# Two attention loops of a graph network: destinations' terms issued in the middle of a group, the rescaling factor issued behind the next sixteen slots' first scaling

## The chip, the cores and the metric

The kernel runs on one core of one Trainium2 chip. The metric is the device time of one execution in microseconds (us). Three runs of the kernel before took 5281.35, 5282.95 and 5290.66 us; their median is 5282.95. A profile of one further execution by the hardware profiler shows every instruction of the five engines: TensorE (PE, with its weight loads listed apart as PEld), VectorE (DVE), ScalarE (ACT), GpSimd (POOL) and SyncE (SP).

## The reference

The kernel computes four layers of a graph network over 3125 nodes with 256 features and 50,000 edges that are sorted by destination. Each layer normalises x, adds a graph part and a dense mixing part, and then a feed-forward part:

```python
edge_index = jnp.stack([src, dst])
xn = _layernorm(x, axis=-1)
x = x + _L0_gnn_ref(xn, edge_index, ...) + _L0_mix_ref(xn[None], ...)[0]
x = x + _L0_ffn_ref(_layernorm(x, axis=-1)[None], ...)[0]
...
```

The change touches the graph parts of layers 0 and 2 alone, which are graph attention: 4 heads of 64 features in layer 0, 8 heads of 32 in layer 2. Node features are multiplied by W, giving h. Each edge has, per head, a score: the source's term (h times att_src, summed over the head's features) plus the destination's term (h times att_dst), through a leaky ReLU of slope 0.2. A softmax over all edges that arrive at one node turns scores into weights, and the node's output is the weighted sum of the sources' h. A softmax needs each destination's maximum before the exponentials; that is what most of the loop below is about.

## The kernel before

**How the work is tiled.** The function `gat` holds the whole attention of one layer. The edges lie in 416 slots of 128 edges (one edge on each partition), each slot's edges having their destinations within one block of 128 nodes. Four slots make a group (`G` = 4, 104 groups), sixteen slots make a block of the loop (`J` = 16, 26 of them, four groups each; `b` is the block, `i` the group's place in it, 0 to 3). The sums for all nodes stay in SBUF in `agg`.

**What one group does.** `scale(g)` multiplies the group's gathered rows of h by the edges' weights (L836, DVE, one instruction of 128x1024; it reads the weights `weighed` from PSUM), copies the weights beside them (L837, ACT) and makes the one-hot matrices of the destinations (L556, DVE). `sums(g)` multiplies one-hot by rows, one matmul a slot (L845, PE), into a ring of PSUM tiles `g`, of which layer 0 has four and layer 2 three. `fetch(g + ring)` issues four gathers (L549, POOL, one indirect DMA a slot) of a later group. `add(g - 1)` adds the PSUM tiles of the group before to `agg` (L574, DVE).

**What one block of sixteen slots needs ahead of its first scaling.** Three pieces are prepared one and two blocks ahead:
- `terms(k)` gives the destinations' terms of half a block (eight slots): a DMA loads the destination rows into `dr` (L726, queued on SP; one buffer), DVE compares them into a transposed one-hot `ohT` (L729; one buffer), ACT copies eight pieces of the terms into `stage` (L732) and PE multiplies eight times (L735) into the PSUM tile `pd`. In layer 0 the two halves of `pd` and both blocks' `weighed` share one PSUM bank; in layer 2, with twice the heads, each half has a bank of its own (`per` is 2 and 1). `terms` for block b + 2 is issued in groups 0 and 1 of block b.
- `ready(b)` adds the three pieces that each term is split into (L743, DVE; L745, ACT) and loads the block's marks. It is issued in group 2, for block b + 2.
- `chain_of(b)` finds the running maximum over the sorted edges and ends in the weights. It is a generator with four stops: first the gathered sources' terms are copied together (L763, ACT, which needs the block's gathers landed), turned, scanned and turned back (L765 to L773); then the scan of the borders (L778 to L790); then the maxima (L794 to L800); then the exponential (L814, ACT), its copy into the PSUM tile `weighed` (L815, ACT) and the marks of the last edges (L816, DVE). Behind the last stop comes one instruction, L820 on DVE: the factor `goes`, by which the partial sum of a destination that continues from one block into the next must be rescaled, because the maximum may have grown. It reads the exponential.

`goes` is used in the first group of the next block: `sums` multiplies it with a one-hot matrix (L850, PE), and `add` applies the product to `agg` (L858 and L860, DVE) ahead of that block's first additions.

**What sets the order.** A scheduler gives each engine its list of instructions by the order of issue in the program text, and adds the semaphore waits. Each engine then runs its own list in that order: an instruction that waits holds everything behind it on its engine. So the places of the calls in the main loop of `gat` are the order written out by hand. After each group that is not the twelfth, `next(steps)` issues one step of the layer's dense mixing part (lines around L471, L473, L1049 to L1073 in layer 0, L1252 to L1267 in layer 2) into the same lists, to fill the holes.

In the kernel before, one turn of the main loop issues: `scale(g)`; in groups 2 and 3 one piece of the next block's chain; `sums(g)`, `fetch`, `add(g - 1)`; in group 1 the chain is started; in groups 1, 2 and 3 another piece of the chain, in group 3 the one that holds L820 alone; then in groups 0 and 1 `terms`, in group 2 `ready`; then a step of the mixing part.

Of the kernel before, what the change touches and what calls it, by code (L numbers as in the profile page):

```python
# [53 lines left out]
def bc(ap, shape):  # L54

    idx, full = [], []
    own = list(ap.shape)
    for n in shape:
        if n is None:
            idx.append(slice(None))  # L60
            full.append(own.pop(0))
        else:
            idx.append(None)
            full.append(n)
    assert not own
    return ap[tuple(idx)].to_broadcast(full)


class Net:
# [592 lines left out]
    def gat(self, pool, pre, H, tiny, side, ring, deg=None, after=None, head=None):  # L662
# [28 lines left out]
        nb, gb, ng = NS // J, J // G, NS // G  # L691
        state = {}
        heads = agg[:, :, :D].rearrange("p t (h c) -> p t h c", h=H)
        with ExitStack() as own:
# [15 lines left out]
            shares = [rp.tile([P, J + 1, 2 * H + 1], F32, name=f"alpha{i}") for i in range(2)]  # L710
# [10 lines left out]
            def terms(k):  # L721

                t0 = k * n
                dr = pool.tile([P, n, P], BF16, name="dr", bufs=1)
                rows = self.dl_rows[t0:t0 + n]
                nc.sync.dma_start(dr, bass.AP(tensor=rows.tensor, offset=rows.offset,  # L726
                                                           ap=[[0, P], [P, n], [1, P]]))
                ohT = pool.tile([P, n, P], BF16, name="ohT", bufs=1)
                nc.vector.tensor_scalar(ohT, dr, self.row, None, op0=ALU.is_equal)  # L729
                rows = pool.tile([P, n, 6 * H], BF16, name="stage")  # L730
                for j, r in enumerate(self.blocks_of(t0, n, ET.Activation)):
                    nc.scalar.copy(rows[:, j, :], dmf[:, bass.ds(r * (6 * H), 6 * H)])  # L732
                pd = pdt[k % 2 // per][:, k % per]
                for j in range(n):
                    nc.tensor.matmul(pd[:, j].rearrange("p s h k -> p (s h k)"), ohT[:, j, :], rows[:, j, :],  # L735
                                     start=True, stop=True)

            def ready(b):

                pds = pool.tile([P, J + 1, 2, H], F32, name="pds")  # L740
                for i, t in enumerate(pdt):
                    m = per * n
                    nc.vector.tensor_reduce(pds[:, i * m:(i + 1) * m], t.rearrange("p a j s h k -> p (a j) s h k"),  # L743
                                            axis=AX.X, op=ALU.add)
                nc.scalar.copy(pds[:, J], pds[:, 0])  # L745
                marks = rp.tile([M, 5 * P], F32, name="marks", bufs=2)
                rows = self.marks[b * J:(b + 1) * J]
                nc.sync.dma_start(marks, bass.AP(tensor=rows.tensor, offset=rows.offset,
                                                 ap=[[5 * P, J], [0, H], [1, 5 * P]]))
                state["in", b] = pds, marks  # L750
# [72 lines left out]
            def fetch(g):  # L823
                if g >= ng:
                    return
                msg = msgs.tile([P, G, W], F32, name="msg")
                for j in range(G):
                    self.gather(msg[:, j, :D + H], htab, g * G + j)
                state["msg", g] = msg

            def scale(g):
                msg = state["msg", g]
                b, s = g // gb, g % gb * G
                al_ = state["w", b][0]
                mh = msg[:, :, :D].rearrange("p j (h c) -> p j h c", h=H)
                nc.vector.tensor_tensor(mh, mh, bc(weighed[b % 2][:, s:s + G], [None, None, None, C]), ALU.mult)  # L836
                nc.scalar.copy(msg[:, :, D:], al_[:, s:s + G])  # L837
                state["oh", g] = self.one_hot(pool, g)

            def sums(g):  # L840
                oh, msg = state.pop(("oh", g)), state.pop(("msg", g))
                out = []
                for j in range(G):
                    q = ps.tile([P, 512], F32, name="g", bufs=room)[:, :W]
                    nc.tensor.matmul(q, oh[:, j, :], msg[:, j, :], start=True, stop=True)  # L845
                    out.append(q)
                state["q", g] = out
                if g and g % gb == 0:
                    q = mm()
                    nc.tensor.matmul(q[:, :H], oh[:, 0, :], state["w", g // gb][1], start=True, stop=True)  # L850
                    state["less"] = q[:, :H]

            def add(g):
                if g and g % gb == 0:
                    less = state.pop("less")
                    at = agg.rearrange("p t w -> p (t w)")[:, bass.ds(self.block_of(g * G, ET.DVE) * W, D + H)]
                    ah = at[:, :D].rearrange("p (h c) -> p h c", h=H)
                    nc.vector.scalar_tensor_tensor(ah, bc(less, [None, None, C]), 1.0, ah, op0=ALU.add, op1=ALU.mult)  # L858
                    ad = at[:, D:]
                    nc.vector.scalar_tensor_tensor(ad, less, 1.0, ad, op0=ALU.add, op1=ALU.mult)  # L860
                self.add_group(agg, g, state.pop(("q", g)))
# [10 lines left out]
            for g in range(ng):  # L872
                b, i = divmod(g, gb)
                scale(g)
                if i > 1 and b + 1 < nb:
                    next(links)
                sums(g)
                fetch(g + ring)
                if g:
                    add(g - 1)  # L880
                if i == 1 and b + 1 < nb:
                    links = chain_of(b + 1)
                if i and b + 1 < nb:
                    next(links, None)
                if b + 2 < nb:
                    if i < 2:
                        terms(2 * (b + 2) + i)
                    elif i == 2:
                        ready(b + 2)
                if g % 12:  # L890
                    next(steps, None)
            add(ng - 1)
# [1709 lines left out]
```

## Time and profile before

| | us |
|---|---|
| median of three runs | 5282.95 |
| the profiled execution's own time | 5287.8 |
| its span, first to last instruction | 5286.0 |
| busy in the span: PE, DVE | 4213.0, 3243.5 |
| busy in the span: POOL, ACT | 2038.9, 1470.6 |
| loop of layer 0, about 155 to 757 of the span | 602 |
| loop of layer 2, about 2930 to 3563 of the span | 633 |
| L836 in both loops, 208 instructions of 1.211 each | 252.0 |
| L845 in both loops, 1664 matmuls of 0.453 each | 576.9 |
| L549 in both loops, 832 gathers of 0.997 each | 829.4 |

The TensorE clock that the throttle granted was 0.883 of full speed on average over the span, 0.89 in layer 0's loop and 0.93 in layer 2's. "Idle before" or "waits" means time in which an engine had nothing running, put down to whatever released the next instruction: `DVE msg L836 <- PE pd L735` is DVE standing still ahead of line 836, which makes `msg`, until line 735 on PE, which writes `pd`, was done. In the timeline each line has the start in the span, the duration, engine, line, operation and tiles, and in square brackets the engine's idle time ahead of it. The two loops do not overlap each other or the rest of the program by more than their edges.

### The profile page before, as it was taken

Reading aid. Unit: us, or ns where it says so; the run is one execution under the profiler, and the core shown is the slowest. Engines: PE = TensorE matmul, PEld = TensorE weight load, DVE = VectorE, ACT = ScalarE, POOL = GpSimd, SP = SyncE. Lnnn points to the kernel's source line nnn. Section 1 sums busy time; section 2 is a strip of 40 time slices with the busy share of each in tenths; the row PEclk is TensorE's granted clock in tenths of the full one; section 3 lists DMA queues with packets and bytes.
Section 4 is the critical chain, followed back from the end, with each engine's and each line's share of the span. In section 5 each row is a group of like instructions: output and inputs, shape, how many; then the busy total and the mean of one; then the engine's idle time right before and its main releaser. Section 6 shows DMA issues by size and latency. Waiting matters only on the chain. (4 is left out here: it accounts for less than half of the span.)

```text
span 5286.0 us, 70446 instructions
## 1 busy us (share of the span) xinstructions
PE 4213.0 (80%) x20470; PEld 3023.8 (57%) x20470; DVE 3243.5 (61%) x7881; ACT 1470.6 (28%) x4893; POOL 2038.9 (39%) x2048
## 2 busy tenths in 40 slices
PE   4788864977777766776795688886999999995996
PEld 2444534864654344554683444555756777775996
DVE  6888787137898467997415787887565443473112
ACT  2323334232100322334222333325342111112232
POOL 1766631426777266771241666641020000001221
PEclk8888885987897788887797799998999999997998
DMA  4544433664454256773464444431023542345554
GB/s 118 137 116 111 113 85 105 190 164 129 144 154 144 74 176 191 226 228 110 128 192 131 126 122 120 118 107 47 6 86 91 184 115 72 87 121 180 175 171 156
DMA packets 395084, 693.86 MB, mean 131 GB/s; under 512 B 88252, under 2 KB 230342, under 8 KB 394689
## 3 DMA queue, kind: packets, MB, share of 16 engines
q1 hardware_dynamic: 288594, 414.48, 25.3%
q0 software_dynamic: 95744, 264.11, 18.0%
q10 hardware_dynamic: 10351, 10.60, 0.6%
q8 instruction: 176, 2.88, 0.2%
q14 instruction: 219, 1.79, 0.1%
HBM read 572.82 MB, written 116.15 MB: 130 GB/s over the span
## 5 line engine op out<-in xcount | busy, mean ns | idle before, releaser
L549 POOL DMA_INDIRECT msg<-L_gnn_htab,src x832 | 829.4, 997 | 566.4 <-issue 332.5
L549 POOL DMA_INDIRECT msg<-L_gnn_c_tab,src x832 | 823.8, 990 | 451.0 <-issue 321.1
L617 PE MATMUL g<-msg,oh 128*128 128x256 f32 x1664 | 554.3, 468 | 267.2 <-DVE agg L574 162.0
L574 DVE TENSOR_TENSOR agg<-agg,g 128x256 f32 (+2 forms) x1664 | 697.5, 419 | 110.3 <-PE g L617 55.6
L845 PE MATMUL g<-msg,oh 128*128 128x265 f32 (+1 forms) x1664 | 576.9, 453 | 131.9 <-DVE agg L574 102.1
L617 PEld LDWEIGHTS g<-msg,oh 128*128 128x128 f32 x1664 | 341.4, 227 | 415.4 <-DVE agg L574 229.7
L1605 DVE COPY y<-y 128x256 f32<-128x256 f32 x162 | 68.8, 425 | 714.9 <-PE y L1602 714.9
L845 PEld LDWEIGHTS g<-msg,oh 128*128 128x128 f32 x1664 | 302.0, 207 | 325.4 <-DVE agg L574 221.9
L1561 POOL DMA_INDIRECT xr<-L_ffn_rows,takes x162 | 155.8, 962 | 791.5 <-PE tx L1570 401.9
L1589 PE MATMUL h<-xe,w 128*128 128x128 f32 x3456 | 418.7, 278 | 2.7 <-DMA w<-in_L_ffn_W 2.7
L1593 ACT ACTIVATE hT<-h,br 128x128 f32<-128x128 f32 x864 | 247.1, 368 | 618.2 <-issue 548.0
L1602 PE MATMUL y<-w,hT 128*128 x1728 | 416.2, 389 | 0.0
L1589 PEld LDWEIGHTS h<-xe,w 128*128 128x128 f32 x3456 | 405.4, 194 | 3.4 <-issue 3.2
L2286 DVE CAST ar<-a 128x640 fp32r<-128x640 bf16 x500 | 254.0, 509 | 223.2 <-PE dn L2288 219.1
L2288 PE MATMUL dn<-ha,ar 128*128 128x512 f32 x1500 | 383.7, 407 | 5.1 <-DVE ha L2253 3.4
L1602 PEld LDWEIGHTS y<-w,hT 128*128 128x128 f32 x1728 | 314.9, 190 | 55.4
L2288 PEld LDWEIGHTS dn<-ha,ar 128*128 128x128 f32 x1500 | 279.0, 189 | 82.5 <-issue 8.9
L836 DVE TENSOR_TENSOR msg<-msg,pd 128x1024 f32<-128x1024 f32 x208 | 252.0, 1211 | 36.9 <-PE pd L735 27.1
L2288 PE MATMUL dn<-hb,ar 128*128 128x512 f32 x1000 | 258.9, 413 | 13.4 <-DVE ar L2286 13.4
L2219 ACT ACTIVATE T<-mm 128x512 bf16<-128x512 f32 (+1 forms) x280 | 151.1, 550 | 361.1 <-PE mm L2217 360.9
L1407 POOL IOTA slot<- 128x56 f32 x3 | 0.9, 294 | 637.9 <-ACT ha L2382 561.7
L1606 POOL DMA_INDIRECT back<-y,puts x162 | 160.6, 991 | 179.6 <-DVE y L1605 138.5
(734 smaller groups left out, 7213.4 us busy)
## 6 DMA issues: line engine op xcount, KB each, us to landing
a<-counted SPq DMA_DIRECT2D x500, 160.0 KB
w<-in_L_ffn_W SPq DMA_DIRECT2D x124, 512.0 KB
w<-in_L_ffn_W SPq DMA_DIRECT2D x62, 1024.0 KB
counted<-T SPq DMA_DIRECT2D x40, 800.0 KB
dr<-dl_rows SPq DMA_DIRECT2D x104, 256.0 KB
heavy_oh<-oh SPq DMA_DIRECT2D x104, 256.0 KB
oh<-heavy_oh SPq DMA_DIRECT2D x104, 256.0 KB
msg<-L_gnn_htab,src POOLq DMA_INDIRECT x832
```

Source lines behind the costliest of these rows:

```text
L549: self.nc.gpsimd.indirect_dma_start(out=out, out_offset=None, in_=table, in_offset=bass.IndirectOffsetOnAxis(ap=self.src[:, t:t + 1], axis=0))
L574: self.nc.vector.tensor_tensor(at, at, q[j], ALU.add)
L617: self.summed = self.nc.tensor.matmul(r, oh[:, j, :], msg[j], start=True, stop=True)
L836: nc.vector.tensor_tensor(mh, mh, bc(weighed[b % 2][:, s:s + G], [None, None, None, C]), ALU.mult)
L845: nc.tensor.matmul(q, oh[:, j, :], msg[:, j, :], start=True, stop=True)
L1561: nc.gpsimd.indirect_dma_start(out=xr, out_offset=None, in_=tab, in_offset=bass.IndirectOffsetOnAxis(ap=takes[:, t:t + 1], axis=0))
L1589: nc.tensor.matmul(q[:, i, :], d["w1"][:, k, c * P:(c + 1) * P], d["xe"][:, k, :], start=(k == 0), stop=(k == 1))
L1593: nc.scalar.activation(hT[:, c, :], q[:, i, :], act, bias=d["br"][:, c:c + 1])
L1602: nc.tensor.matmul(q, d["hT"][:, c, :], w2f[:, bass.ds(e * (nh * D) + c * D, D)], start=False, stop=(c == nh - 1))
L1606: s = nc.gpsimd.indirect_dma_start(out=self.back, out_offset=bass.IndirectOffsetOnAxis(ap=puts[:, t:t + 1], axis=0), in_=y, in_offset=None)
L2286: nc.vector.tensor_copy(r, a)
L2288: nc.tensor.matmul(q.rearrange("p i f -> p (i f)"), r[:, k, :], of(h, k0 + k).rearrange("p i f -> p (i f)"), start=(k0 + k == 0), stop=(k0 ...
```

## The change

Three things change in `gat`. `scale` takes the block's weights from the list `shares` by the block's number, where it took them from the record that the last piece of the chain leaves; it is the same tile. The last piece of the chain, the factor `goes` (L820), is issued in group 0 of the next block, behind that group's `scale`, where it was issued at the end of group 3 ahead of it. And `terms` is issued between `scale` and `sums` of groups 0 and 1, where it was issued at their end, behind `sums`, `fetch` and `add`. The pieces of the chain in groups 1, 2 and 3 and `ready` in group 2 stay where they were.

```diff
@@ scale(g)
                 msg = state["msg", g]
                 b, s = g // gb, g % gb * G
-                al_ = state["w", b][0]
+                al_ = shares[b % 2]
@@ the main loop
                 scale(g)
                 if i > 1 and b + 1 < nb:
                     next(links)
+                elif b and i == 0:
+                    next(links, None)
+                if i < 2 and b + 2 < nb:
+                    terms(2 * (b + 2) + i)
                 sums(g)
                 fetch(g + ring)
                 if g:
                     add(g - 1)
                 if i == 1 and b + 1 < nb:
                     links = chain_of(b + 1)
-                if i and b + 1 < nb:
-                    next(links, None)
-                if b + 2 < nb:
-                    if i < 2:
-                        terms(2 * (b + 2) + i)
-                    elif i == 2:
-                        ready(b + 2)
+                if i in (1, 2) and b + 1 < nb:
+                    next(links)
+                if i == 2 and b + 2 < nb:
+                    ready(b + 2)
                 if g % 12:
                     next(steps, None)
```

## The prediction

> **What bounds the kernel now.** First the page's busy shares and its chain of what ended last, to see whether the two attention loops matter; then busy time in the stretch of each loop; then what DVE, PE, ACT and POOL wait for in those stretches; last the timeline of one block's turn in each. The page and the two stretches:
>
> ```profile
> span 5286.0 us, 70446 instructions
> PE 4213.0 (80%) x20470; PEld 3023.8 (57%) x20470; DVE 3243.5 (61%) x7881; ACT 1470.6 (28%) x4893; POOL 2038.9 (39%) x2048
> ...
> 155.00:757.00 602.00, 499.39 (x2078) 276.66 (x2078) 493.85 (x1199) 186.87 (x844) 374.97 (x383) 0.89 0.42 114
> 2930.00:3563.00 633.00, 522.60 (x2240) 320.11 (x2238) 519.84 (x1289) 203.07 (x979) 382.68 (x384) 0.93 0.44 119
> ```
>
> In the two lower lines the columns are length, then busy time of PE, weight loads, DVE, ACT and POOL, clock, DMA share, GB/s. Layer 0's loop takes 602 us and layer 2's 633, together 1235 of 5286; only they change. In both PE and DVE are each busy 82 to 83%: neither bounds alone. They hand work to each other, and a wait of one tells only if the other has nothing queued. The waits of DVE (total, times, longest), layer 0 above, layer 2 below:
>
> ```profile
> DVE msg L836 <- PE pd L735: 26.2, 22, 3.4
> DVE goes L820 <- ACT alpha L814: 9.2, 7, 3.1
> ...
> DVE goes L820 <- ACT alpha L814: 47.8, 22, 3.9
> DVE ohT L729 <- DMA dr<-dl_rows: 1.2, 3, 0.5
> DVE msg L836 <- PE pd L735: 0.8, 2, 0.6
> ```
>
> The two waits that the change is next to: the scaling L836 held by the terms' matmuls L735 (layer 0 alone, where both halves of the terms and the factors `weighed` are in one PSUM bank; layer 2 has two banks and 0.8 us), and the rescaling factor L820 held by the exponential L814 (layer 2 above all). One turn of a block in layer 2:
>
> ```profile
> 3227.09 0.22 ACT L763 COPY mine<-msg 128x32 f32<-128x32 f32 x1 [3.18 <-DMA msg<-L_gnn_htab,src]
> ...
> 3228.11 0.31 ACT L814 ACTIVATE alpha<-z 128x136 f32<-128x136 f32 x1
> 3228.45 0.17 DVE L820 SCALAR_TENSOR_TENSOR goes<-alpha,goes 128x8 f32<-128x8 f32 x1 [1.58 <-ACT alpha L814]
> 3228.68 0.26 ACT L815 COPY pd<-alpha 128x128 f32<-128x128 f32 x1
> 3229.22 1.21 DVE L836 TENSOR_TENSOR msg<-msg,pd 128x1024 f32<-128x1024 f32 x1
> 3231.45 0.33 PEld L850 LDWEIGHTS mm<-goes,oh 128*128 128x128 f32 x1
> ```
>
> L836 needs L815, which ends at 3228.94, 0.52 us after L814. So the exponential that L820 waits for is also on the way to L836. And ACT itself is late because the gather's landing is (3.18 us). That is a cycle: L836 opens the old block's last sums, these free the buffers of POOL's next gathers, they land, and the next exponential follows. A block takes 24.9 us here, 24.0 in layer 0, with 25 turns each.
>
> **The change part by part.** Instruction for instruction the five engines run what they ran before (104 calls of `terms`, 52 factors); only the order moves. The scaling's other name for the factor tile costs nothing, it is the same tile.
>
> *The terms, moved ahead of the sums, layer 0.* A call of `terms` issues one 256 KB DMA on SP's queue, one DVE compare L729 (0.48 us), eight ACT copies L732 (0.21 us each) and eight matmuls L735. They used to stand at the end of groups 0 and 1, so the next group's scaling came soon behind them and had to wait out the same bank: DVE stood 26.2 us, 22 times. In the new order, on PE the first half's L735 run right after the old block's last four sums matmuls, before the group's own sums; the second half's after the sums of the block's first group. On DVE the work between the second half's compare and the following scaling rises from 1.3 us to about 3.5; between the first half's and its scaling it is 0.7 to 1.6, as now. So the second half's wait goes and the first half's is shortened only by what PE no longer has ahead of it. From the present stalls, block by block, I estimate 0.2 to 0.45 us a block left over; 25 x 0.44 = 11. Term: 11 - 26.2 = -15 (bounds -26.2, all gone, and 0, where sums that are late take its place on PE).
>
> Ahead of this stands PE: its sums wait for the adds (50.4 us, 75 times), so L735 in that place uses PE time that was often idle; eight take 0.35 us in one row of the timeline, with 0.47 of weight loads beside them. If PE had no hole there, it would be 50 x 0.5 = 25 us the other way, and I keep that for the range.
>
> *The terms' DMA.* The destination rows have one buffer, so the next load is issued when the compare L729 has read it. Measured from issue to landing in the trace it takes 3.05 to 4.07 us, mostly about 3.5. Now 4.1 to 8.6 us of DVE work stand between the two compares, and the wait is 1.2 us in layer 2 and absent in layer 0. In the new order I count only 3.1 us of it in 9 blocks of layer 0 and 3.1 to 3.8 in 6 of layer 2. Each then waits 0.3 to 0.5 us: 9 x 0.45 = +4 and 6 x 0.35 = +2 (bounds 0, and 15 x 1.0, the slowest landing less the shortest work: +15). The page "DMA: Bandwidth & Descriptors" of the Trainium skill, section "Anatomy of one DMA", would fit 2.0 us plus bytes over 436 GB/s, an estimate of 2.6 us for 256 KB, on the gpsimd path; by it nothing would wait, this term would be 0 and the forecast 5266. Its rule "issue the DMA early, wait late" (section "Rules for kernel authors") speaks against the change, which pulls the two compares together. The trace's 3.5 us decides.
>
> *The factor L820, behind the first scaling.* DVE no longer stands at L820; it stands at L836 instead, until L815 is done 0.26 to 0.5 us after L814, and what stood between the two (side work, an add) is run during the wait. Going through the blocks with the trace's own end times, the stall sum is 11.8 -> 10.9 us in layer 0 and 52.1 -> 49.5 in layer 2 (both include short stalls that the list puts elsewhere). Terms -0.9 and -2.6, instead of the -57.0 that the list of waits would promise.
>
> Queued behind the moved L820 is PE's L850, which multiplies the factor, and behind it the group's side matmuls. The factor is now done 1.21 + 0.17 = 1.38 us or more after the scaling starts. L850 needs the one-hot L556 too, which comes after the scaling both before and after (it is what PE waits for: 5.1 us in layer 2), so mostly L850 was not ready earlier. It bounds at 0 and 25 x 1.38 = +34.5; I take 0, nearest to the row above, where L850 runs 2.2 us after L836's start, and later than the factor would be.
>
> *The terms in layer 2.* No bank is shared, so nothing is gained at L836 (0.8 us at most). What counts is whether L735 delays the old block's last sums, which release POOL. By the order on PE, the eight stand ahead of the last of them in some of the block patterns: +0.5 us in two, +0.8 in three, -1 in two where a side matmul moves behind, the rest unchanged. Over the loop that is -3 to +5: +1.
>
> Sum: layer 0, -15 + 4 - 0.9 = -11.9; layer 2, -2.6 + 2 + 1 = +0.4; together -11.5. The profiled execution took 5287.8 us (span 5286.0 and 1.8 around it), so 5276.3 for it; the median of the three runs is 4.85 lower, so **5271.5, say 5272 us**. About 0.2%, 10.6 us, is what a measurement of this kernel can tell from no change: the forecast is at that edge.
>
> **The rivals.**
> *The waits only change hands: 5283.* For it: L820's wait does so by the working above, and PE and DVE being busy 83 and 82% means that a stall taken from DVE can come back as a stall of PE on the adds (50.4 us now). Against it: 26.2 us of one wait at one bank are not work. It gives -11.5 + 11.5, no change.
>
> *All of it is gained: 5249.* The wait of 26.2 goes entirely, layer 0's 0.9 too, and in layer 2 the scaling starts as L815 ends, 0.28 us earlier a block as in the timeline, and the whole cycle with it: 25 x 0.28 = 7. 34 off: 5253.8 - 4.85. Against it: the first half has no more cover on DVE than now.
>
> *Slower: 5306.* The place is layer 2's turn of a block. PE is in order; L850 waits for the factor 1.38 us after the scaling's start, and terms and sums behind it wait too, so that the gathers' release is late by as much in each of 25 blocks: +34.5 - 11.9 = +22.6. For it: POOL sat idle in 5 us pieces there and ACT waits 63.5 us on landings, so the cycle has no slack. Against it: the one-hot, which L850 needs as well. It cancels layer 0's gain from 0.48 us a block on, and is slower past the bound from 0.9.
>
> **How the numbers follow.** Likeliest case, partial gain (5260 to 5283): 0.38, of which 0.23 below 5272.4, 0.12 within the bound and 0.03 past it, where the transfer's bound of +15 comes in. All gained: 0.18. Hands changed: 0.14. Slower by the cycle or by PE's missing hole: 0.30. Hence faster 0.41, within 0.26, slower 0.33. The range reaches into the full gain and the slower case, 5246 to 5306; the likeliest one's own is 5260 to 5283.
>
> **What the profile after would show.** In layer 0 the wait of L836 on L735 falls from 26.2 to about 11; near 26 says that the move does not get the matmuls out of the way, near 0 the full gain. The wait of L820 on L814 vanishes in both loops and a wait of L836 on L815 of about 45 to 50 us stands in layer 2; if it is far under 40, the cycle has become shorter than I think. L729 waits on its DMA for 4 to 8 us where it was 1.2. Layer 2's length tells the slower rival: 633 -> 650 or more, with POOL's idle time grown and PE waiting at L850 on L820. The prediction is wrong if the stall taken from DVE in layer 0 appears on PE, L845 on L574, above 60.

## The result and the profile after

The changed kernel took 5298.51 us (median of 8 runs, 5285.72 to 5311.52), the kernel before 5283.25 us in the 8 runs beside it (5267.59 to 5298.72). The ratio is 1.0028 with a 95% interval of 1.0015 to 1.0042: some 15 us slower, where 11 us faster was forecast. The profiled execution of after took 5311.5 us, the longest of its eight; the first of the two lines below is the page's, the others are busy time in the two loops, each from its first scaling L836 to its last (length, then PE, weight loads, DVE, ACT, POOL, granted clock, DMA share, GB/s).

```profile
span 5309.7 us, 70468 instructions
...
157.80:766.60 608.80, 509.57 (x2079) 279.86 (x2080) 496.20 (x1202) 187.28 (x848) 380.02 (x383) 0.87 0.42 113
2949.90:3589.20 639.30, 525.41 (x2237) 329.21 (x2235) 517.56 (x1288) 202.06 (x978) 380.38 (x384) 0.91 0.43 118
```

Between the same instructions, layer 0's loop took 603.5 us before and 608.8 after, layer 2's 631.7 and 639.3: +5.3 and +7.6. Of the profiles' difference of 23.7 us another 11.0 lie between the loops (2172.3 and 2183.3 us), where the change moves nothing; so one execution differs from the next by that much. The loops' 12.9 are near the 15 of the medians, but each is one execution. DVE does the same work as before (496 and 518 us). PE is busy 10 us longer in layer 0, with the same matmuls, at a granted clock of 0.87 where it was 0.89.

The waits of DVE, then of PE, in layer 0's loop after; then of DVE and of PE in layer 2's (total, times, longest). The windows are those of the two lines above:

```profile
DVE msg L836 <- PE pd L735: 17.1, 16, 4.0
DVE msg L836 <- ACT pd L815: 13.0, 11, 3.1
...
DVE ohT L729 <- DMA dr<-dl_rows: 2.0, 5, 0.5
...
PE g L845 <- DVE agg L574: 62.0, 83, 4.0
...
DVE msg L836 <- ACT pd L815: 22.6, 9, 4.4
DVE goes L820 <- ACT alpha L814: 19.8, 7, 4.7
...
DVE ohT L729 <- DMA dr<-dl_rows: 4.0, 7, 1.1
...
PE pd L735 <- DVE ohT L729: 14.1, 7, 3.4
...
PE mm L850 <- DVE goes L820: 6.0, 6, 2.0
```

Before, PE's rows for the same two waits were, in layer 0's loop and in layer 2's:

```profile
PE g L845 <- DVE agg L574: 50.4, 75, 2.2
...
PE pd L735 <- DVE ohT L729: 2.0, 2, 1.1
```

In layer 0 the scaling's wait for the terms fell from 26.2 to 17.1 us, and PE's wait for the adds rose from 50.4 to 62.0. In layer 2 the wait for the exponential is split between L820 and L836, 42.4 us together, where it was 48.1 before (47.8 at L820, 0.3 at L836). New is PE standing at L735: 14.1 us on L729, where before it stood 2.0. These matmuls now have sums behind them.

The lists that the engines run do not follow the order of issue alone, as I had it ahead of the change: the scheduler places instructions earlier or later than the program text does. So the edit moves less than it says. In layer 2 the factor L820 still runs ahead of the scaling in 7 of 25 turns (in layer 0 in 3), and these 7 are the whole 19.8 us. Of the 48 calls of `terms` in a loop, the first L735 runs 2 to 8 of the sums' matmuls earlier than before in 45 calls of layer 0, but only in 27 of layer 2, there by 2 to 6.

Where the longest blocks come from is seen in one place of the timeline. After, the turn into block 11 of layer 2 (POOL's idle time at the end counts from its last gather):

```profile
3227.22 0.22 ACT L763 COPY mine<-msg 128x32 f32<-128x32 f32 x1 [4.89 <-DMA msg<-L_gnn_htab,src]
3227.35 0.38 ACT L1253 ACTIVATE qk<-mm 128x256 f32<-128x256 f32 x1
...
3228.21 0.17 DVE L1254 TENSOR_SCALAR s<-s 128x2 f32<-128x2 f32 x1 [4.63 <-ACT qk L1253]
3228.36 0.44 DVE L574 TENSOR_TENSOR agg<-agg,g 128x273 f32 x1
...
3228.86 1.28 PE L845 MATMUL g<-msg,oh 128*128 128x273 f32 x2 [3.83 <-DVE agg L574]
...
3234.32 2.08 PE L473 MATMUL mm<-L_mix_W_qkv,xT 128*128 128x512 f32 x2
...
3238.05 0.94 POOL L549 DMA_INDIRECT msg<-L_gnn_htab,src  x1 [8.48 <-issue]
```

ACT stands 4.89 us at a copy L763, which waits for a gather to land. Behind it in ACT's list is a square of the mixing part, behind that in DVE's list an add, and behind that PE's sums: all four stop. PE then runs at half clock (two of the matmuls L473 take 2.08 us; four of them took 1.98 at 3220.86, at full clock). The stretch in the middle has the clock in the last column but two:

```profile
3220.00:3228.00 8.00, 4.88 (x17) 2.56 (x17) 3.49 (x12) 1.30 (x8) 5.99 (x7) 1.00 0.62 176
...
3232.00:3238.00 6.00, 6.00 (x13) 3.34 (x12) 1.91 (x4) 0.00 (x0) 0.00 (x0) 0.50 0.00 0
```

PE is busy all of these 6 us and POOL has nothing, since the old block's sums, which free its buffers, come through at half speed. Its next gather starts 9.26 us after the scaling (6.90 in the same block before), so it lands late, and the next L763 waits for such gathers. Blocks 5 and 11 take 29.6 and 29.8 us, before 26.5 and 26.8.

### The profile page after: what moved, and what is told of

Its sections match the earlier page's. It is cut to its first block, busy times and chain, and to the rows that moved or that the text cites. A ratio compares the mean times of both kernels' runs of the same rounds, so it can differ in the third digit from the quotient of the medians.

```text
span 5309.7 us, 70468 instructions
## 1 busy us (share of the span) xinstructions
PE 4234.7 (80%) x20470; PEld 3041.7 (57%) x20470; DVE 3242.7 (61%) x7881; ACT 1469.1 (28%) x4893; POOL 2041.0 (38%) x2048
## 3 DMA queue, kind: packets, MB, share of 16 engines
q1 hardware_dynamic: 288594, 414.48, 25.3%
## 5 line engine op out<-in xcount | busy, mean ns | idle before, releaser
L836 DVE TENSOR_TENSOR msg<-msg,pd 128x1024 f32<-128x1024 f32 x208 | 252.1, 1212 | 55.5 <-ACT pd L815 35.6
L2289 PEld LDWEIGHTS dn<-hb,ar 128*128 128x128 f32 x1000 | 192.8, 197 | 65.9 <-DVE ar L2287 21.9
```

What stands on the lines that cost most here:

```text
L2289: nc.tensor.matmul(q.rearrange("p i f -> p (i f)"), r[:, k, :], of(h, k0 + k).rearrange("p i f -> p (i f)"), start=(k0 + k == 0), stop=(k0 ...
```

## The experiments

Ratios are to the kernel before on the same chip, with 95% intervals. Loops are from the first to the last scaling, of one profiled execution each; executions of one loop that nothing was changed in differ by up to 9 us (layer 2 unchanged: 631.7 and 623.0), so a smaller difference of single loops says little. "Half clock" is the time in layer 2's loop at a granted clock of 0.5.

| kernel | ratio | layer 0 | layer 2 | half clock |
|---|---|---|---|---|
| before | 1 | 603.5 | 631.7 | 82 |
| after | 1.0028 [1.0015, 1.0042] | 608.8 | 639.3 | 110 |
| e1 terms alone | 1.0020 [1.0007, 1.0033] | 596.3 | 638.6 | 99 |
| e2 factor alone | 0.9978 [0.9967, 0.9990] | 605.6 | 608.9 | 59 |
| e3 both, layer 0 alone | 1.0000 [0.9986, 1.0014] | 595.0 | 623.0 | 80 |
| e4 both, layer 2 alone | 1.0034 [1.0015, 1.0053] | 607.3 | 651.8 | 136 |
| e5 after, L735 behind the sums | 1.0002 [0.9992, 1.0012] | 586.9 | 631.5 | 89 |
| e6 factor, terms in layer 0 | 0.9961 [0.9948, 0.9975] | 596.4 | 606.8 | 54 |
| e7 after, L763 behind L814 | 0.9878 [0.9863, 0.9894] | 590.4 | 590.5 | 61 |
| e8 factor, L763 behind L814 | 0.9860 [0.9845, 0.9875] | 591.9 | 583.7 | 51 |
| e13 after, step shifted | 1.0050 [1.0032, 1.0068] | 599.5 | 641.5 | 109 |
| e14 factor, step shifted | 1.0034 [1.0021, 1.0048] | 600.7 | 644.0 | 132 |
| e15 before, L763 behind L814 | 0.9874 [0.9854, 0.9894] | 591.3 | 588.1 | 59 |
| e16 e6, L763 behind L814 | 0.9871 [0.9851, 0.9891] | 593.8 | 586.6 | 54 |

**Which part.** e1 moves the terms alone, e2 the factor alone; e3 and e4 do both in one loop.

```diff
 e1, on before
                     next(links)
+                if i < 2 and b + 2 < nb:
+                    terms(2 * (b + 2) + i)
                 sums(g)
...
-                if b + 2 < nb:
-                    if i < 2:
-                        terms(2 * (b + 2) + i)
-                    elif i == 2:
-                        ready(b + 2)
+                if i == 2 and b + 2 < nb:
+                    ready(b + 2)
 e2, on after: the same lines the other way
 e3 and e4, on after: the two moves only where moved is true
+            moved = H == 4        # e4: H == 8
```

> Only the terms are moved between the scaling and the sums; the factor L820 stays at the end of the block's last group. Theory A (the terms' matmuls, now ahead of the sums on PE, make the sums wait for the compare L729 and the copies L732): this alone gives nearly the whole loss, +10 to +16 us on before, and PE's waits of L735 on L729 and of L845 on L732 stand as in the changed kernel (14 us in layer 2, 5 us in layer 0). Theory B (the loss is the factor's new place): 0 to -10 us. Theory C (no single part: every reordering that lengthens PE's holes lowers the granted clock): the half-clock time grows with the loss.

> Only the factor L820 is moved behind the next block's first scaling; the terms stay at the end of groups 0 and 1. Theory A: -4 to +3 us on before. Theory B (L850 waits for the factor, and what stands behind it): +10 to +16 us, with PE's wait of L850 on L820 at 6 us or more.

> Both parts in layer 0's loop alone, where before the scaling waited 26 us on the terms' matmuls in the shared bank. My forecast of the place had -12 us here. From the profile of the changed kernel, whose loop is 5 us longer than before, +5 us; if the time of the loops' surroundings is noise, then layer 0 alone is +3 to +7 us.

> Both parts in layer 2's loop alone, where nothing waits on a shared bank. From the profile of the changed kernel, whose loop is 7.6 us longer, +6 to +10 us; with the run before it the sum of the two should be the loss of the changed kernel, +15 us.

The terms alone cost 11 us of 5286.3 (interval 4 to 17), the factor alone gains 12 (5 to 17). So theory B falls, and the loss is the terms'. By layer, e3 is no change (+3 to +7 was expected) and e4 is +18 us (8 to 28; 6 to 10 was expected): the loss is layer 2's. But theory A had 14 us of PE at L735 on L729 in layer 2 for e1 too, and there it is 6.4. The waits that carry this, of e2 in layer 2 (its L820 and L836 as in the changed kernel):

```profile
DVE msg L836 <- ACT pd L815: 17.9, 8, 3.3
DVE goes L820 <- ACT alpha L814: 17.8, 9, 3.4
...
PE pd L735 <- DVE ohT L729: 2.4, 2, 1.5
```

With the factor alone DVE stands 35.7 us for the exponential, where it stood 48.1 before (47.8 at L820, 0.3 at L836), and layer 2's loop is 23 us shorter. In e4 both parts in the same loop give 651.8. The two parts don't add: the factor gains where the terms stay, and loses its gain where they move. Theory C's sign is there in the first six rows: layer 2's half-clock time, 59 to 136 us, goes up and down with its loop. e1 speaks against a loss by the squares qk of the mixing part (the narrow form of theory D, below): there none of them stands behind L763, and layer 2's loop is as long as the changed kernel's (638.6 and 639.3).

**Is it L735 ahead of the sums?** e5 leaves the load, the compare and the copies of the terms in the new place and issues the eight matmuls behind the sums again. e6 moves the factor in both loops and the terms in layer 0 alone.

```diff
 e5, on after: terms becomes a generator
                 for j, r in enumerate(self.blocks_of(t0, n, ET.Activation)):
                     nc.scalar.copy(rows[:, j, :], dmf[:, bass.ds(r * (6 * H), 6 * H)])
+                yield
                 pd = pdt[k % 2 // per][:, k % per]
...
                 if i < 2 and b + 2 < nb:
-                    terms(2 * (b + 2) + i)
+                    rest = terms(2 * (b + 2) + i)
+                    next(rest)
                 sums(g)
...
                 if i in (1, 2) and b + 1 < nb:
                     next(links)
+                if i < 2 and b + 2 < nb:
+                    next(rest, None)
 e6, on after: early = H == 4; terms ahead of sums where early, else at the end
```

> The changed kernel with each terms call cut in two: its load, compare L729 and copies L732 stay between the scaling and the sums, its eight matmuls L735 go back behind the sums, the additions and the chain's piece. Theory A (the loss is L735 ahead of the sums on PE): the loss of +15 us goes, 0 to -10 us on before, and PE's wait of L735 on L729, 14 us in layer 2, falls under 4. Theory D (the loss is on ACT: in blocks 5 and 11 of layer 2 the side work's squares qk now stand behind the four copies L763, which wait for gathers that land late, and DVE, PE and POOL follow): ACT's list has the same place for them here, so +10 to +16 us stays.

> The factor behind the first scaling in both loops, the terms moved in layer 0 alone. The profiles of the runs so far have layer 0's loop at about 600 us with the terms moved and 605 without, and layer 2's at 609 with the factor alone: -12 to -18 us on before. If the terms' place is bad in either loop, it is no better than the factor alone: -11.

e5 is at 1.0002: the loss is gone, as theory A has it, and the gain of the factor has not come back. But it is a weak test of L735's place. In PE's list the matmuls run later than in the changed kernel in only 8 of 48 calls of layer 2 and in 10 of layer 0. PE's wait at them on L729 in layer 2 fell from 14.1 to 6.4 us, not under 4, and its wait at L850 on L820 rose from 6.0 to 12.1. Layer 2's loop, 631.5, is still 22.6 above e2's. And most of the shortening stands in layer 0's loop (608.8 to 586.9), where e3 shows no loss; no run explains that. So L735's place can be one part of the loss, and how large a part stays open. e6 is 0.9961, 21 us faster than before (13 to 28), the best ratio that the two moves give, though its interval overlaps e2's.

e6 and the changed kernel differ only in the terms of layer 2: 0.9961 against 1.0028, each to the kernel before on its own chip. So the terms' new place costs some 35 us there (25 to 45) once the factor is moved.

**Is it the queue behind L763?** In ACT's list the next block's four copies L763 stand ahead of the exponential L814 of the block at hand, though they are issued later in the program: in layer 2 in nearly every block, before and after, in layer 0 in a few early blocks and in all but the last from the eleventh on. The timeline shows ACT held there by landings. The row before, in layer 2's loop:

```profile
ACT mine L763 <- DMA msg<-L_gnn_htab,src: 63.5, 23, 4.1
```

In the changed kernel two of the four squares qk stand behind them in blocks 5 and 11 besides. e7 and e8 turn the order of L763 and L814 round, in after and in e2, and compute the same:

```diff
                 nc.vector.scalar_tensor_tensor(zs, zs, 0.2, zs, op0=ALU.mult, op1=ALU.max)
-                z = pool.tile([P, J + 1, H], F32, name="z", bufs=1)
+                z = mine[:, 0]
                 nc.vector.tensor_tensor(z, zs[:, 0], zs[:, 1], ALU.subtract)
```

L814 now reads `mine`, and L763, which writes it, can't go before.

> The changed kernel, but the exponential's input z is written into the tile mine where it had a tile of its own, so that the next block's four copies L763, which overwrite mine, must stand behind L814 on ACT, where now they stand ahead of it and hold it until late gathers have landed. The same work, nothing left out. Theory D: the waits of the factor and of the scaling on ACT (48 us in layer 2) go nearly all, layer 2's loop falls by 30 to 50 us, and the terms' place does no more harm: -30 to -50 us on before. Theory A: L735 ahead of the sums costs what it cost, so at best half of that. If the gathers' cycle is bound by POOL and not by L814: within 10 us of the changed kernel.

> The same order on ACT, with the factor alone moved and the terms where they were before. Theory D: as the run before it, -30 to -50 us on before, within 5 us of it. Theory A: 10 to 20 us faster than the run before it.

Both are much faster than before: -65 and -74 us of 5289.5, more than theory D had. ACT in the same phase of layer 2 in e8, and its waits in that loop:

```profile
3175.86 0.32 ACT L814 ACTIVATE alpha<-mine 128x136 f32<-128x136 f32 x1 [0.43 <-DVE mine L812]
...
3178.55 0.22 ACT L763 COPY mine<-msg 128x32 f32<-128x32 f32 x1 [0.27 <-DMA msg<-L_gnn_htab,src]
```

```profile
ACT alpha L814 <- DVE mine L812: 62.8, 19, 7.5
...
ACT mine L763 <- DMA msg<-L_gnn_htab,src: 35.1, 19, 4.8
...
DVE msg L836 <- ACT pd L815: 2.9, 4, 1.0
```

The exponential waits for its own input and no longer for the next block's gathers; DVE's wait for ACT, 48 us before, is 2.9. Layer 2's loop falls to 583.7 with half-clock time at 51 us. ACT still waits 35.1 us for gathers, but behind the exponential. The cycle that the prediction named (landing, exponential, scaling, sums, POOL's buffers, landing) was held together by a place in ACT's list, and is cut by one line.

e13 and e14 test the squares qk by themselves, by a shift of one step of the mixing part in layer 2:

```diff
+            ahead = (1,) if H == 8 else ()
...
                 if i == 1 and b + 1 < nb:
                     links = chain_of(b + 1)
+                if g % 12 and i in ahead:
+                    next(steps, None)
...
-                if g % 12:
+                if g % 12 and i not in ahead:
                     next(steps, None)
```

These two and the order for before (e15) and for e6 (e16) first fell on a chip where the kernel before took 5815.89 us and the part between the loops was longer too (2467 to 2473 us in these four profiles, not 2172). There they gave 0.9911 [0.9891, 0.9930], 0.9998 [0.9977, 1.0018], 0.9971 [0.9958, 0.9983] and 0.9948 [0.9929, 0.9967], with loops of 671 to 741 us. What held for the other chips did not hold there: the shifted step in the changed kernel gained most, and the order gave far less than the 65 to 74 us above. The traces have only half as many completions of DMAs as the others (27 thousand, not 55), and why the chip differs stays open. Their expectations were:

> The changed kernel, but in layer 2 the side work's step of each block's group 1 is issued between the chain's start and its first piece, no longer at the end of the group. By the list that ACT gets, the squares qk, which in the changed kernel stand behind the four waiting copies L763 in blocks 5 and 11, now stand ahead of them in every block. Theory D: blocks 5 and 11 fall from 29.6 and 29.8 us to about 25, the loop of layer 2 by 10 to 15 us, so 0 to +5 us on before. Theory A (L735 ahead of the sums): the loop stays at about 640, +10 to +16 us.

> The same shift of the step in layer 2, with the factor alone moved and the terms where they were before. Here ACT's list gets the squares qk behind the four copies L763 in blocks 5, 6, 11 and 12, where with the factor alone they stood ahead. Theory D: these four blocks rise from about 24.5 us to 28 to 30, layer 2's loop from 609 to 625 to 630, so 0 to +8 us on before although the terms are not moved. Theory A: as with the factor alone, -11 us.

> The kernel before with z in the tile mine, so that L763 stands behind L814 on ACT; neither the factor nor the terms are moved. Theory D: the factor's new place saved DVE a wait that came from L763; with that gone it saves little, so this is within 5 us of the same order with the factor moved (5216.75, -73 on before).

> The order with L763 behind L814, the factor moved in both loops, the terms in layer 0 alone. If the terms' harm that is left with this order (10 us between the two runs that had it) is in layer 2, this is as fast as the factor with that order, or up to 5 us faster: -73 to -78 us on before. If it is in layer 0: -60 to -65.

On a chip like the first ones (before: 5294.86 us):

> The changed kernel with layer 2's step of group 1 ahead of the chain's first piece, on another chip than the first time, where the kernel before took 5815.89 us and the gathers of all layers were slower. Theory D (the squares qk behind the four waiting copies L763 in blocks 5 and 11): blocks 5 and 11 fall from 29.6 and 29.8 us to about 25, layer 2's loop from 639 to 625 to 629, 0 to +5 us on before. Theory A (L735 ahead of the sums): the loop stays at about 640, +10 to +16 us.

> The factor alone moved, with that step's shift, which here puts qk behind the four copies L763 in blocks 5, 6, 11 and 12, where with the factor alone they stood ahead. Theory D: these four blocks rise from about 24.5 us to 28 to 30, layer 2's loop from 609 to 625 to 630: 0 to +8 us on before although the terms are not moved. Theory A: as with the factor alone, -11 us.

> The kernel before with z in the tile mine, so that L763 stands behind L814 on ACT; neither the factor nor the terms are moved. If the factor's new place only saved DVE a wait that came from L763: within 5 us of the same order with the factor moved (-73 us on before). If it is worth its 11 us by itself: about -62.

> L763 behind L814, the factor moved in both loops, the terms in layer 0 alone. If the 10 us that the terms' place still costs in that order is in layer 2: -73 to -78 us on before. If it is in layer 0: -60 to -65.

In e13 blocks 5 and 11 fell to 26.4 and 24.9 us, as theory D said, but the loop stayed at 641.5, as theory A said: other blocks rose (block 2 from 24.5 to 27.4, block 7 from 25.9 to 27.3). In e14 two of the squares qk stand behind L763 in blocks 5, 6, 11 and 12, which rose by about 1 us at most (to 25.3, 24.7, 25.4, 25.3) and not to 28, and yet the loop went from 609 to 644 with the terms in their old place. The times, +26 us (17 to 36) and +18 us (11 to 25), are above what either theory had. So D falls in its narrow form: qk behind L763 can lengthen blocks 5 and 11, as in the changed kernel, but it is not the rule. Moving one side step costs this loop as much as moving the terms.

e15 and e16 with e7 and e8 give the wider form. With L763 behind L814 the four arrangements (neither moved, factor moved, factor and half the terms, both) are at 0.9874, 0.9860, 0.9871 and 0.9878 with intervals that overlap, and layer 2's loop is 583.7 to 590.5. With L763 ahead, the kernels above spread it from 607 to 652. e7 and e16 differ only in the terms of layer 2, as the changed kernel and e6 do: the 35 us there are 4 here, within the intervals. Between e8 and e7, on one chip, the medians differ by 10 us (5216.75 and 5227.00, four runs each). So the new places of the terms and of the factor have little price of their own, some 10 us at most; nearly all of their effect in layer 2, in both directions, comes through the late gathers that ACT waits for ahead of the exponential. That it is ACT's list is seen in e15's trace: in layer 2's loop DVE, PE and POOL run their instructions in the order of the kernel before (six matmuls and six gathers fall on the other side of the loop's start), and only ACT's order differs. In layer 0 the one line turns the lists of PE and DVE too, so its 12 us there (603.5 to 591.3, against 631.7 to 588.1 in layer 2) are not shown to be this order's alone. These four beat both kernels and can hardly be told from each other, so the smallest edit, e15, one line in the kernel before, is as good a choice: 0.9874, 67 us (56 to 77).

## Why the prediction was wrong

- **Sign.** 5272 was forecast and 5298.51 measured; that is inside the range but on the other side. The step that failed is "the terms in layer 2", +1 with bounds -3 to +5: it measured about +35 with the factor moved (the changed kernel against e6; in single executions of the loop 30 to 45, 651.8 and 639.3 against 608.9 and 606.8), and +7 to +16 in e1's loop without the factor. I counted which matmuls stand ahead of the last sums, by their own 0.5 to 0.8 us, and not what they wait for: L735 stood 14.1 us for L729, and with it the sums. What made a delay of the sums so dear was the place of L763: with that turned round the same move costs 4 us, within the intervals (e7 against e16). How the 35 us divide between PE's wait and the rest of the cycle stays open.
- **The terms in layer 0**, -15: right in sign, too large. The wait fell by 9.1 us, not 15, and PE's wait for the adds rose by 11.6 to 62.0, past the 60 that was named as the sign of failure. ACT's wait for landings in this loop rose from 10.5 to 27.2 us. With the terms moved the loop is 599.2 us on the mean of five executions (after, e1, e3, e6, e13), without 604.3 on the mean of four (before, e2, e4, e14): -5. In the medians, e6 against e2 is 0.9961 against 0.9978, with intervals that overlap.
- **The terms' DMA**, +6: right in size as a wait; what it cost in time no run separates. All waits of L729 on it in the whole execution went from 1.7 us in 4 to 7.9 in 14. The page "DMA: Bandwidth & Descriptors" of the Trainium skill, section "Anatomy of one DMA", whose fit had none of it, is for the gpsimd path; this load is on SP's queue.
- **The factor**, -3.5: right in sign, mis-sized; alone it measured -12 (5 to 17). I kept every other time as it was when I moved the stall. In e2's layer 2 PE's wait for the adds falls from 48.9 to 44.6 us and the half-clock time from 82 to 59; that the one brings the other is argued. Nor did the wait at L820 vanish in both loops: the scheduler left L820 ahead of the scaling in 7 of layer 2's 25 turns, and 19.8 us stand there. At L836 it is 22.6, far under the 40 that was named, and yet the cycle had not become shorter.
- **L850 behind the factor**, 0, with +34.5 as the far end: nearly right. PE stands there 6.0 us, 6 times, in layer 2 after, and e2 moves the factor too and is faster. The slower rival came true at 5298.5 for 5306, but not by its mechanism: L850 waits 6.0 us and L735 14.1. That the number came close is luck.
- **The rival that waits only change hands** describes layer 0 best: +0.0 in e3 (-7 to +7).
- **A block** takes 25.0 us in layer 2 and 23.8 in layer 0 on the mean of the 25 turns before, where I had 24.9 and 24.0; nothing hangs on it.

What no step had is the multiplication. Windows of 3.4 us in which PE idled 1.8 us or more were nearly always followed by half clock (the table below); in block 11 the sums that free POOL's buffers then ran slower, and the next gather started later. And I read the 63.5 us of ACT on landings as the gathers being late, when it was a copy that stood in the wrong place of ACT's list. That row was among the waits before, with the exponential directly behind the copy in the timeline.

## What to carry to other kernels

When a wait on a late transfer stands in front of a critical instruction only by its place in an in-order list, look at that place first: here one reused buffer, which forced the order, gave 67 us, and two careful moves around it changed the time by -21 to +18. This loop answered to every reordering tried, also to a shift of side work, so a move judged there by its own cost is judged wrongly. Read the engines' lists from the trace of the kernel, not from the program text: the scheduler had put copies ahead of an exponential that is issued before them, and moved fewer instructions than the edit asked for. And of instructions that are moved ahead on an engine, count what they wait for, not how long they run.

## What the runs showed of the hardware

PE's granted clock in these loops is either full or half, and half in stretches of 3.4 us and multiples of it, at a fixed phase. Cutting both loops of seven profiles (before, after, e1, e2, e5, e7, e8) into such windows of 3.41 us at full clock, the following window was at half clock:

| PE idle in the window | followed by half clock |
|---|---|
| under 0.6 us | 2 of 1175 |
| 0.6 to 1.2 | 30 of 554 |
| 1.2 to 1.8 | 109 of 241 |
| 1.8 and more | 108 of 110 |

The ends of matmuls are modelled in the profile, so the idle times are rough. The page "TensorE: Matmul & The Clock Gate" of the Trainium skill, section "What's actually happening", has free-running windows of 3413 ns, which agrees, and the fall to half clock after an idle window; here a window that is half idle was enough. In the kernel before, PE spent 133 us of layer 0's loop and 82 of layer 2's at half clock. That the half clock causes part of the loss, rather than going with it, is argued from block 11 and from PE's 10 us more of busy time in layer 0; no run changed the clock alone.
